# Two hyperbolic graph layers: four shared PSUM slots and two tiles per turn

## The chip, the cores and the metric

The kernel runs on one core of a Trainium2 chip. The metric is the device time in microseconds of one execution; for the kernel before the median of three runs is 863.87 us (863.44 to 865.81). The profile is of one further execution with a span of 859.7 us from first to last instruction.

## What is computed

Four graph layers run one after another on a node matrix `x` of 3327 x 64 with a 3327 x 3327 adjacency of zeros and ones. Each layer normalises the rows, cuts them at zero, applies a graph operation and adds its result to `x`. Layers 0 and 3 are hyperbolic and are the ones that the change touches. Cut to what matters (layer 0, c = 1):

```python
h = relu(layernorm(x))
left, right = logmap0(h) @ W[:64] + b, logmap0(h) @ W[64:]
att = sigmoid(left + right.T) * adj
local = logmap(h[:, None, :], h[None, :, :])       # 3327 x 3327 x 64 in the reference
x = x + proj(expmap(h, einsum('ij,ijd->id', att, local)))
```

The logarithmic map is a function of scalar products of two nodes times one of the two node vectors. So the kernel never builds the 64 components for a pair: it makes one number per pair of nodes, multiplies it by the attention weight, and sums it against the node vectors with matmuls.

## The kernel before

Rows are padded to 3328 = 26 x 128. In the kernel `T` is 26, `HT` 13 and `D` 64. `hyperbolic_series` is called twice: for layer 0, with the adjacency from memory in f32, and for layer 3, with masks in fp8 that layer 1 left on the chip. It has three stages: a preparation, a loop over pairs of nodes, and an end that makes the new `x`.

**Preparation** (L344 to L436). It normalises, makes `Xr` (scaled node vectors), splits it into f16 parts `hi` and `lo` beside nine columns `F` in the tile `Xp`, and transposes it 128 rows at a time with `to_columns16` into `XT` (high and low parts, one column per node). `Xe` and its transpose `XE` hold the other operand. `left` and `right` are the two terms of the attention; `left` is split into three bf16 parts and transposed into `LT`. `table_of` (L424) loads the sigmoid's function table.

**Loop** (L442 to L601). The result's columns are cut into four chunks: `(0, 4)`, `(4, 3)`, `(7, 3)`, `(10, 3)`, each of so many blocks of 128 columns in both halves of the nodes. A chunk is 2 x 512 or 2 x 384 columns wide, and for each chunk all 26 row blocks are gone through. So there are 26 wide tiles (128 x 1024) and 78 narrow ones (128 x 768) per loop. The order on the four computing engines is written out by hand, one tile a turn. Per tile, by name and line:

- `products` on TensorE, L519 and L520: four f16 matmuls make `L` in PSUM, from `XT` and `XE` (stationary) and from `XC` and `XF` (moving);
- `square` on ScalarE, L526: `y` from `L`;
- `sigmoid` on ScalarE, L504, from `leftB` (the chunk's `left`, the same in all partitions), then on GpSimd, L512, times the adjacency; in layer 0 the diagonal block of the adjacency is first cleared by `drop_diagonal` (L178), for 26 of the 104 tiles;
- `weights` on VectorE, L530 and L531: `L` becomes a series value, then `sig` becomes `L * sig`;
- `sums` on TensorE, L537: `sig` against `Xr`, summed over the 26 row blocks in PSUM; L545: after every second tile the same against `X0` for both tiles.

[...] `L` has two buffers of two banks each, so a tile's products wait until L531 of the tile two before has read its buffer. The two accumulators of a chunk take one bank each and have two buffers each. In turn k TensorE does `sums(k-2)` and then `products(k+1)`; ScalarE `square(k)` and `sigmoid(k+2)`; VectorE `weights(k)`.

What a chunk begins with is made in the turns before it: `columns` copies `XT` into `XC` by two DMAs (L473); `begin` spreads `left` over the partitions with matmuls (L480) into the coming chunk's accumulators, `begin2` copies that to `leftB` (L486) and transposes `Xp` into the same banks (L488), `begin3` copies that to `XF` (L494) and in layer 0 makes a part of `diag` on GpSimd (L497). What a chunk ends with is spread over turns after it: `out_of` (L554) copies the sums, `back` (L560) transposes them, `to_m` and `to_m2` (L567 to L576) reduce them.

Adjacency tiles come through SyncE's DMA queue (`load`, L467), with four buffers, issued three tiles ahead of the sigmoid. The same queue issues the `XC` copies.

Of the kernel before, what the change touches and what calls it, by code (L numbers as in the profile page):

```python
# [9 lines left out]
F32 = mybir.dt.float32  # L10
# [36 lines left out]
def tile_gnn4(ctx: ExitStack, tc: tile.TileContext, x, adjT, att0, b0, w1, bias1, w_gat, a_gat,  # L47
# [133 lines left out]
    def move(tp, hs, x2, m, s, q, r, min_norm2, um, maxn2, isqc):  # L181
# [80 lines left out]
        if isqc is not None:  # L262
# [8 lines left out]
    pick = const.tile([3 * T, T], BF, name="pick")  # L271
    V.memset(pick, 1.0)
    G.affine_select(out=pick, in_=pick, pattern=[[-3, T]], compare_op=OP.is_ge, fill=0.0,
                    base=0, channel_multiplier=1)
    G.affine_select(out=pick, in_=pick, pattern=[[3, T]], compare_op=OP.is_ge, fill=0.0,
                    base=2, channel_multiplier=-1)
# [31 lines left out]
    def hyperbolic_series(r, params, ok, masks=None, done=None):  # L308
# [15 lines left out]
        KE = D + 9  # L324
        W = 512
        with ExitStack() as st:
# [7 lines left out]
            XE = pers.tile([KE, NP], F16, name="XE")  # L334
            Xp = pers.tile([P, T, 2 * D + 9], F16, name="Xp")
            hi, lo, F = Xp[:, :, :D], Xp[:, :, D:2 * D], Xp[:, :, 2 * D:]
            LT = pers.tile([3 * T, P], BF, name="LT")
# [4 lines left out]
            wlr, bcol, cc, sqc, isqc, um, maxn2 = params  # L342

            with tc.tile_pool(name="hsp", bufs=1) as tp, tc.tile_pool(name="hsps", bufs=2, space=PSUM) as ps:  # L344
                A.memzero(X0)
                Xe = tp.tile([P, T, KE], F16, name="Xe")
                E = Xe[:, :, D:]
                V.memset(E[:, :, 6:], SX)
                for k, part in enumerate(f16_parts((1.0 - 2.0 * G1) * SX)):
                    V.memset(F[:, :, 6 + k:7 + k], part)  # L350
# [31 lines left out]
                root_ = sqrt_(tp, root, "zs")  # L382
                for ts in HALVES:
                    V.scalar_tensor_tensor(lo[:, ts, :], Xr[:, ts, :], SX, hi[:, ts, :], op0=OP.mult, op1=OP.subtract)  # L384
# [11 lines left out]

                to_columns16(XT, Xp[:, :, :2 * D], P, 1)

# [24 lines left out]
                pl = parts3(left, "pl", BF)  # L423
                table_of(AF.Sigmoid, root[:, :1])  # L424
                pe = ps.tile([P, 4 * P], F32, name="pe", bufs=1)
                PE.matmul(pe[:3 * T, :P], pl.rearrange("p t k -> p (t k)"), ident_bf, start=True, stop=True)
                A.activation(LT, pe[:3 * T, :P], AF.Copy)
                V.tensor_mul(right, lr[:, :, 1], z)
                V.tensor_scalar(right, right, bcol, None, op0=OP.add)
                for k, src in ((0, p0), (3, hm0), (5, h0)):  # L430
                    V.tensor_scalar(F[:, :, k:k + src.shape[-1]], src, -1.0, None, op0=OP.mult)
                to_columns16(XE, Xe, KE, 0)
# [9 lines left out]
            with tc.tile_pool(name="hsw", bufs=2) as wk, tc.tile_pool(name="hsps", bufs=2, space=PSUM) as ps, \  # L442
                    tc.tile_pool(name="hsacc", bufs=2, space=PSUM) as pa, \
                    tc.manual_schedule(engines={mybir.EngineType.Activation, mybir.EngineType.DVE,
                                                mybir.EngineType.PE, mybir.EngineType.Pool}):
                HT = T // 2
                tiles = [(c, b) for c in ((0, 4), (4, 3), (7, 3), (10, 3)) for b in range(T)]
                K = len(tiles)
                XC, XF = {}, {}
                acc, leftB, adjs, sigs, Ls, ys, later = {}, {}, {}, {}, {}, {}, {}  # L450

                def halves(t, c):

                    return t.rearrange("p (o i) -> p o i", o=2)[:, :, c[0] * P:(c[0] + c[1]) * P]
# [14 lines left out]
                def columns(c):  # L469

                    XC[c] = new("XC", c, F16)
                    for o in range(2):
                        nc.sync.dma_start(XC[c][o * D:(o + 1) * D, :, :], halves(XT[:D, :], c))  # L473

                def begin(c):
                    acc[c] = [pa.tile([P, W], F32, name=f"acc{o}") for o in range(2)]
                    for o in range(2):
                        for i in range(c[1]):
                            t = o * HT + c[0] + i
                            PE.matmul(acc[c][o][:, i * P:(i + 1) * P], pick[:, t:t + 1].to_broadcast([3 * T, P]), LT,  # L480
                                      start=True, stop=True)

                def begin2(c, o):
                    if o == 0:
                        leftB[c] = new("leftB", c)
                    A.activation(leftB[c][:, o, :], acc[c][o][:, :c[1] * P], AF.Copy)  # L486
                    for i in range(c[1]):
                        PE.matmul(acc[c][o][:KE, i * P:(i + 1) * P], Xp[:, o * HT + c[0] + i, D:], ident_h,  # L488
                                  start=True, stop=True)

                def begin3(c, o):
                    if o == 0:
                        XF[c] = new("XF", c, F16, KE)
                    A.activation(XF[c][:, o, :], acc[c][o][:KE, :c[1] * P], AF.Copy)  # L494
                    if masks is None:
                        t0 = o * HT + c[0]
                        G.tensor_tensor(diag[:, t0 * P:(t0 + c[1]) * P].rearrange("p (t i) -> p t i", i=P),  # L497
                                        ident[:, None, :].to_broadcast([P, c[1], P]),
                                        dcol[:, t0:t0 + c[1], None].to_broadcast([P, c[1], P]), op=OP.mult)

                def sigmoid(k):
                    c, b = tiles[k]
                    sig = sigs[k] = new("sig", c, bufs=6)
                    A.activation(sig, leftB[c], AF.Sigmoid, bias=right[:, b:b + 1])  # L504
                    if masks is None:
                        adj = adjs.pop(k)
                        t = b % HT - c[0]
                        if 0 <= t < c[1]:
                            drop_diagonal(adj[:, b // HT, t * P:(t + 1) * P], 0, 0, P)
                    else:  # L510
                        adj = halves(masks[b // 2][:, b % 2, :], c)
                    G.tensor_tensor(sig, adj, sig, op=OP.mult)  # L512

                def products(k):
                    c, b = tiles[k]
                    rows = slice(b * P, (b + 1) * P)
                    L = Ls[k] = ps.tile([P, 2, W], F32, name="L")[:, :, :c[1] * P]
                    for o in range(2):
                        PE.matmul(L[:, o, :], XT[:, rows], XC[c][:, o, :], start=True, stop=False)  # L519
                        PE.matmul(L[:, o, :], XE[:, rows], XF[c][:, o, :], start=False, stop=True)  # L520

                def square(k):

                    c, b = tiles[k]
                    ys[k] = new("y", c)
                    A.activation(ys[k], Ls[k], AF.Square, scale=-0.5 / SX ** 2, bias=shift_c)  # L526

                def weights(k):
                    L, y, sig = Ls.pop(k), ys.pop(k), sigs[k]
                    V.scalar_tensor_tensor(L, y, G3, L, op0=OP.add, op1=OP.mult)  # L530
                    V.tensor_mul(sig, L, sig)  # L531

                def sums(k):
                    c, b = tiles[k]
                    n = c[1] * P
                    for o in range(2):
                        PE.matmul(acc[c][0][o * D:(o + 1) * D, :n], Xr[:, b, :], sigs[k][:, o, :],  # L537
                                  start=b == 0, stop=b == T - 1)
                    if b % 2 == 1:

                        for i in range(2):
                            w = sigs.pop(k - 1 + i)
                            for o in range(2):
                                q = 32 * (2 * i + o)
                                PE.matmul(acc[c][1][q:q + 32, :n], X0[:, b - 1 + i, :], w[:, o, :],  # L545
# [994 lines left out]
```

## Time and profile before

| | |
|---|---|
| median of 3 runs | 863.87 us |
| span of the profiled execution | 859.7 us |
| VectorE busy | 728.3 us, 85% |
| TensorE busy | 672.2 us, 78% |
| ScalarE busy | 577.1 us, 67% |
| GpSimd busy | 425.7 us, 50% |
| DMA | 104.27 MB, mean 121 GB/s |

A line of the profile's groups names a source line, an engine, an operation, what it writes and reads, and how often it occurs; behind the bar stand the busy time in all, the mean time of one in ns, and the idle time of the engine just before these instructions with the instructions that ended most of it. In the timeline the columns are start, duration, engine, line and operation; brackets hold the idle time before and what ended it. PE is TensorE, DVE VectorE, ACT ScalarE, POOL GpSimd, SP SyncE. Durations of matmuls include the way through the array, so matmuls that follow each other overlap in the timeline, and the distance between starts is what one costs. The same holds, less so, for VectorE and ScalarE.

### The profile page before, as it was taken

Reading aid. Unit: us, or ns where it says so; the run is one execution under the profiler, and the core shown is the slowest. Engines: PE = TensorE matmul, PEld = TensorE weight load, DVE = VectorE, ACT = ScalarE, POOL = GpSimd, SP = SyncE. Lnnn points to the kernel's source line nnn. Section 1 sums busy time; section 2 is a strip of 40 time slices with the busy share of each in tenths; the row PEclk is TensorE's granted clock in tenths of the full one; section 3 lists DMA queues with packets and bytes.
Section 4 is the critical chain, followed back from the end, with each engine's and each line's share of the span. In section 5 each row is a group of like instructions: output and inputs, shape, how many; then the busy total and the mean of one; then the engine's idle time right before and its main releaser. Section 6 shows DMA issues by size and latency. Waiting matters only on the chain.

```text
span 859.7 us, 11940 instructions
## 1 busy us (share of the span) xinstructions
PE 672.2 (78%) x4264; PEld 245.2 (29%) x4264; DVE 728.3 (85%) x1020; ACT 577.1 (67%) x712; POOL 425.7 (50%) x309
## 2 busy tenths in 40 slices
PE   0489998989989219989990997617999899899960
PEld 0312232323322004434440562212222233232220
DVE  7389888889889899998989946795998889888976
ACT  3578878888978237777770306457888789788751
POOL 3289997998989410003110000005777677676730
PEclk9789999999999759999995899957999999999995
DMA  2556666666665428998944530001000000000001
GB/s 41 139 173 194 190 180 172 184 186 184 185 179 148 170 83 302 358 364 308 360 166 169 195 127 1 0 0 23 1 1 10 1 1 10 1 1 1 1 2 43
DMA packets 53877, 104.27 MB, mean 121 GB/s; under 512 B 8016, under 2 KB 30064, under 8 KB 53808
## 3 DMA queue, kind: packets, MB, share of 16 engines
q1 hardware_dynamic: 48704, 103.10, 37.8%
q10 hardware_dynamic: 4656, 0.08, 0.3%
q8 instruction: 35, 0.57, 0.3%
q14 instruction: 34, 0.28, 0.1%
q0 software_dynamic: 448, 0.24, 0.1%
HBM read 100.85 MB, written 0.85 MB: 118 GB/s over the span
## 4 chain that ended last, share of the span: by engine, by line
PE 46%; DVE 35%; ACT 11%; issue 4%; DMA 2%; ACTq 1%; DVEq 0%; SPq 0%; POOL 0%; POOLq 0%
DVE sig L531 11%; DVE L L530 10%; PE cnt L1265 9%; PE acc L537 7%; PE L L519 6%; PE acc L545 6%; ACT y L526 6%; PE acc L1282 5%; PE L L520 5%; PE acc L1378 4%; ACT sig L504 2%; DMA XC<-XT 1%; DVE deg L1397 1%; DVE X L711 1%; PE pt L391 1%
## 5 line engine op out<-in xcount | busy, mean ns | idle before, releaser
L512 POOL TENSOR_TENSOR sig<-mask,sig 128x768 f32<-128x768 fp8e4 (+1 forms) x104 | 174.5, 1679 | 215.7 <-DMA XC<-XT 153.4
L530 DVE SCALAR_TENSOR_TENSOR L<-y,L 128x768 f32<-128x768 f32 (+1 forms) x208 | 213.3, 1025 | 50.0 <-ACT y L526 48.0
L526 ACT ACTIVATE y<-L,shift_c 128x768 f32<-128x768 f32 (+1 forms) x208 | 198.1, 953 | 81.6 <-PE L L520 80.8
L531 DVE TENSOR_TENSOR sig<-L,sig 128x768 f32<-128x768 f32 (+1 forms) x208 | 213.2, 1025 | 21.7
L512 POOL TENSOR_TENSOR sig<-adj,sig 128x768 f32<-128x768 f32 (+1 forms) x104 | 202.6, 1960 | 27.5 <-ACT sig L504 22.4
L504 ACT ACTIVATE sig<-leftB,right 128x768 f32<-128x768 f32 (+1 forms) x208 | 203.7, 980 | 0.0
L537 PE MATMUL acc<-sig,Xr 128*64 128x384 f32 (+1 forms) x832 | 193.0, 542 | 2.1 <-DVE sig L531 2.1
L519 PE MATMUL L<-XC,XT 128*128 128x384 f16 (+1 forms) x416 | 146.5, 352 | 37.8 <-DVE sig L531 27.9
L520 PE MATMUL L<-XF,XE 73*128 73x384 f16 (+1 forms) x416 | 144.7, 348 | 0.0
L1271 ACT ACTIVATE w<-cnt,ebias 128x832 bf16<-128x832 f32 x104 | 93.7, 950 | 30.5 <-PE cnt L1265 30.5
L1178 DVE TENSOR_SCALAR_CACHE_REDUCE same<-adj 128x1664 bf16<-128x1664 f32 x52 | 97.7, 1879 | 3.1 <-DMA adj<-in 3.0
L519 PEld LDWEIGHTS <-XT 128*128 128x128 f16 x416 | 41.1, 99 | 198.1 <-DVE sig L531 154.7
L545 PE MATMUL acc<-sig,X 128*32 128x384 f32 (+1 forms) x832 | 94.2, 525 | 0.0
L1265 PE MATMUL cnt<-mask,after 128*128 128x416 fp8e4 x208 | 54.9, 347 | 23.3 <-DVE mask L1258 20.7
L178 POOL TENSOR_TENSOR mask<-mask,offdiag 128x128 fp8e4<-128x128 fp8e4 x26 | 13.4, 535 | 107.5 <-PE cnt L1265 105.5
L1265 PE MATMUL cnt<-mask,rest 128*128 128x416 fp8e4 x208 | 54.8, 346 | 12.4 <-ACT w L1271 12.4
L537 PEld LDWEIGHTS acc<-sig,Xr 128*64 128x64 f32 x832 | 41.3, 135 | 70.2 <-issue 63.9
L1258 DVE TENSOR_SCALAR mask<-adj 128x1664 fp8e4<-128x1664 f32 x52 | 53.3, 1033 | 1.4 <-DMA adj<-in 1.2
L1282 PE MATMUL acc<-w,h 128*64 128x416 bf16 x416 | 47.1, 349 | 0.0
L520 PEld LDWEIGHTS <-XE 73*128 73x128 f16 x416 | 41.5, 100 | 18.2 <-issue 2.2
L391 PE MATMUL pt<-ident_h,Xp 128*128 128x128 f16 x52 | 5.9, 313 | 41.5 <-DVE Xp L384 41.5
L1378 PE MATMUL acc<-mask,h 128*64 128x416 fp8e4 x416 | 37.9, 344 | 0.3
(295 smaller groups left out, 567.7 us busy)
## 6 DMA issues: line engine op xcount, KB each, us to landing
adj<-in SPq DMA_DIRECT2D x65, 832.0 KB, 6.4
adj<-in SPq DMA_DIRECT2D x78, 384.0 KB, 3.8
adj<-in SPq DMA_DIRECT2D x26, 512.0 KB, 4.7
XC<-XT SPq DMA_DIRECT2D x12, 96.0 KB, 2.6
X<-in SPq DMA_DIRECT2D x1, 832.0 KB, 4.5
out<-X SPq DMA_DIRECT2D x2, 416.0 KB, 2.7
XC<-XT SPq DMA_DIRECT2D x4, 128.0 KB, 5.1
gw<-in POOLq DMA_DIRECT2D x4, 48.0 KB, 6.4
```

The source lines that it names most:

```text
L504: A.activation(sig, leftB[c], AF.Sigmoid, bias=right[:, b:b + 1])
L512: G.tensor_tensor(sig, adj, sig, op=OP.mult)
L519: PE.matmul(L[:, o, :], XT[:, rows], XC[c][:, o, :], start=True, stop=False)
L520: PE.matmul(L[:, o, :], XE[:, rows], XF[c][:, o, :], start=False, stop=True)
L526: A.activation(ys[k], Ls[k], AF.Square, scale=-0.5 / SX ** 2, bias=shift_c)
L530: V.scalar_tensor_tensor(L, y, G3, L, op0=OP.add, op1=OP.mult)
L531: V.tensor_mul(sig, L, sig)
L537: PE.matmul(acc[c][0][o * D:(o + 1) * D, :n], Xr[:, b, :], sigs[k][:, o, :], start=b == 0, stop=b == T - 1)
L545: PE.matmul(acc[c][1][q:q + 32, :n], X0[:, b - 1 + i, :], w[:, o, :], start=b == 1, stop=b == T - 1, tile_position=(0, q))
L1178: V.tensor_scalar(same, adj, 0.0, 0.0, op0=OP.is_equal, op1=OP.add, accum_out=count)
L1265: PE.matmul(cnt[o][:, h, :BK], w, cols(k, o, h), start=w is after and steps[k][1] == T - 1, stop=True, skip_group_check=True)
L1271: A.activation(ws[k][:, o, :, :], cnt[o][:, :, :BK], AF.Exp, scale=-LN2, bias=ebias)
```

## The change

The loop is rebuilt around four PSUM slots of two banks each. At any time one is the running chunk's accumulator (both sums in one slot), up to three hold `L`; at the end of a chunk a slot is used to transpose the sums back. A slot that is done goes to the end of a list, and the next user takes the first. TensorE takes two tiles a turn: the sums of two tiles, then the products of two. A slot more for `L` is to let the products run further ahead of VectorE, and the larger turns to spare changes of operand on TensorE.

What a chunk begins with is no longer made by matmuls and copies in the loop. `XE` gets nine more rows that hold `F`, so that `XF` can be copied from `XT` and `XE` by DMA as `XC` is; `left` is written once to device memory as a row, and `leftB` is read from there into all partitions. The first chunk's operands can't wait for that: `XC` of that chunk is issued as soon as `XT` is whole, its `leftB` and `XF` are made in the preparation by matmuls and transposes, and the first adjacency loads and sigmoid are issued a tile earlier. `left` is transposed in f32 and no longer split. Ten matmuls without use (`keep_busy`) are to hold TensorE's clock up. The sigmoid's function table is loaded earlier.

`drop_diagonal` goes from this loop (for a pair of equal nodes the logarithmic map is zero). `sig` has seven buffers instead of six, `y` three instead of two.

```diff
-    pick = const.tile([3 * T, T], BF, name="pick")
...
+    rows = [nc.dram_tensor(f"left{k}", (T, P), F32, kind="Internal").ap() for k in range(2)]
...
+            def columns(c):
...
+                for o in range(2):
+                    nc.sync.dma_start(XC[c][o * D:(o + 1) * D, :, :], halves(XT[:D, :], c))
+                if c[0]:
+                    nc.sync.dma_start(XF[c][:D, :, :], halves(XT[D:, :], c))
+                    nc.sync.dma_start(XF[c][D:, :, :], halves(XE[KE:, :], c))
+                    nc.sync.dma_start(leftB[c], bass.AP(tensor=left_row.tensor, offset=left_row.offset + c[0] * P,
+                                                        ap=[[0, P], [HT * P, 2], [1, n]]))
...
+                table_of(AF.Sigmoid, root_[:, :1])
...
+                def keep_busy(n):
+
+                    for _ in range(n):
+                        PE.matmul(junk, ident_h, hi[:, :8, :], start=True, stop=True)
+
+                keep_busy(4)
                 to_columns16(XT, Xp[:, :, :2 * D], P, 1)
+                columns(chunks[0])
...
-                pl = parts3(left, "pl", BF)
-                table_of(AF.Sigmoid, root[:, :1])
...
+                PE.transpose(pe[:T, :P], left, ident)
+                A.activation(LT, pe[:T, :P], AF.Copy)
+                nc.sync.dma_start(left_row, LT)
+                c = chunks[0]
+                for o, to in ((0, junk), (1, pe)):
+                    for i in range(c[1]):
+                        t = o * HT + c[0] + i
+                        PE.matmul(to[:, i * P:(i + 1) * P], ident[:T, t:t + 1].to_broadcast([T, P]), LT,
+                                  start=True, stop=True)
+                    A.activation(leftB[c][:, o, :], to[:, :c[1] * P], AF.Copy)
...
-                to_columns16(XE, Xe, KE, 0)
+                G.tensor_copy(F, Fe)
+                to_columns16(XE, Xe, KE + 9, 0)
+                for o in range(2):
+                    pt = ps.tile([P, 4 * P], F16, name="pt", bufs=4)
+                    for i in range(c[1]):
+                        PE.transpose(pt[:KE, i * P:(i + 1) * P], Xp[:, o * HT + c[0] + i, D:], ident_h)
+                    V.tensor_copy(XF[c][:, o, :], pt[:KE, :c[1] * P])
+                keep_busy(6)
...
+                slots = [ps.tile([P, 2, W], F32, name=f"slot{k}") for k in range(4)]
+                made = [0]
...
-                    if masks is None:
-                        adj = adjs.pop(k)
-                        t = b % HT - c[0]
-                        if 0 <= t < c[1]:
-                            drop_diagonal(adj[:, b // HT, t * P:(t + 1) * P], 0, 0, P)
...
+                def products(to):
+
+                    while made[0] < min(to, K) and slots:
+                        k = made[0]
+                        made[0] += 1
+                        c, b = tiles[k]
+                        rows = slice(b * P, (b + 1) * P)
+                        L = Ls[k] = slots.pop(0)
...
                     V.scalar_tensor_tensor(L, y, G3, L, op0=OP.add, op1=OP.mult)
                     V.tensor_mul(sig, L, sig)
+                    slots.append(slot)
...
+                    if b == 0:
+                        acc[c] = slots.pop(0)
...
-                for k in range(-7, K + 10):
-                    if 0 <= k - 2 < K:
-                        sums(k - 2)
-                    if 0 <= k + 1 < K:
-                        products(k + 1)
...
+                for j in range(-1, K // 2 + 5):
+                    for k in (2 * j - 2, 2 * j - 1):
+                        if 0 <= k < K:
+                            sums(k)
+                    for i in range(2):
+                        k = 2 * j + i
+                        products(2 * j + 3 + i)
+                        if 0 <= k < K:
+                            weights(k)
+                        if i == 0 and (j, 0) in later:
+                            later.pop((j, 0))()
+                        products(2 * j + 4)
+                        if k + 2 < K:
+                            square(k + 2)
+                        if k + 3 < K:
+                            if masks is None and k + 5 < K:
+                                load(k + 5)
+                            sigmoid(k + 3)
+                        if i == 1 and (j, 1) in later:
+                            later.pop((j, 1))()
+                    if at(2 * j + 10, 1):
+                        columns(at(2 * j + 10, 1))
...
```

## The prediction

> **What bounds the kernel now.** First the busy shares: three engines are close together, so the page alone names no bound.
>
> ```profile
> PE 672.2 (78%) x4264; PEld 245.2 (29%) x4264; DVE 728.3 (85%) x1020; ACT 577.1 (67%) x712; POOL 425.7 (50%) x309
> PE 46%; DVE 35%; ACT 11%; issue 4%; DMA 2%; ACTq 1%; DVEq 0%; SPq 0%; POOL 0%; POOLq 0%
> ```
>
> The chain of work that ended last is mostly TensorE and VectorE, so I looked at where the two hyperbolic loops lie. By the timeline of VectorE the first runs from 44.11 (first L530) to 282.68 us (end of the last L531), 238.6 us; the second from 590.89 to 829.68, 238.8 us. Together 55% of the span. The changed lines lie in these loops and in the preparation before each.
>
> Next the groups by line, shapes apart: what one tile costs VectorE.
>
> ```profile
> L530 DVE SCALAR_TENSOR_TENSOR L<-y,L 128x768 f32<-128x768 f32 x156 | 149.6, 959 | 22.1 <-ACT y L526 20.3
> L531 DVE TENSOR_TENSOR sig<-L,sig 128x768 f32<-128x768 f32 x156 | 149.5, 958 | 16.3
> L530 DVE SCALAR_TENSOR_TENSOR L<-y,L 128x1024 f32<-128x1024 f32 x52 | 63.7, 1225 | 27.9 <-ACT y L526 27.7
> ```
>
> In the timeline two of these start 1.06 and 0.88 us apart (1.32 and 1.16 for 1024 columns), so VectorE can't do a narrow tile in under 1.94 us or a wide one in under 2.48. A loop has 26 wide and 78 narrow tiles: 64.5 + 151.3 = 216 us, with some 5 us of reductions between chunks 221. The loop takes 18 us more. The timeline of a steady stretch says why:
>
> ```profile
> 803.34 0.34 PE L519 MATMUL L<-XC,XT 128*128 128x384 f16 x1
> 804.11 0.87 PE L537 MATMUL acc<-sig,Xr 128*64 128x384 f32 x4
> 805.26 0.34 PE L519 MATMUL L<-XC,XT 128*128 128x384 f16 x1 [0.29 <-DVE sig L531]
> 806.02 0.87 PE L537 MATMUL acc<-sig,Xr 128*64 128x384 f32 x4
> 806.82 0.85 PE L545 MATMUL acc<-sig,X 128*32 128x384 f32 x8
> 807.60 0.34 PE L519 MATMUL L<-XC,XT 128*128 128x384 f16 x1
> 809.40 0.96 DVE L530 SCALAR_TENSOR_TENSOR L<-y,L 128x768 f32<-128x768 f32 x1 [0.30 <-ACT y L526]
> ```
>
> From start to start: products P 0.77, first sums S 0.80, second sums Z 0.78. A pair of tiles is P S P S Z, 3.92 us of TensorE; VectorE needs 3.88. Four tiles take 8.15 (801.25 to 809.40), 4.075 per pair: TensorE stands ready for P and waits for L531 to free one of only two L buffers (0.29), then P comes late, the square too, and VectorE waits (0.30). Two full engines wait for each other in turn. Wide pairs take 5.145 (10.29 for four). So 13 x 5.145 + 39 x 4.075 = 225.8; the remaining 12.9 us of a loop are its start and three chunk boundaries.
>
> Last the start of the first loop:
>
> ```profile
> 32.57 1.54 SPq L473 DMA_DIRECT2D XC<-XT  x2
> 34.16 6.93 SPq L467 DMA_DIRECT2D adj<-in  x3
> 41.04 0.61 PE L519 MATMUL L<-XC,XT 128*128 128x512 f16 x1 [7.88 <-DMA XC<-XT]
> 44.11 1.23 DVE L530 SCALAR_TENSOR_TENSOR L<-y,L 128x1024 f32<-128x1024 f32 x1 [14.00 <-ACT y L526]
> ```
>
> Everything stands from 33 to 41 us because XC was issued behind three adjacency loads of 512 KB. The 0.61 us matmul is one at half clock; the same shape takes 0.38 later.
>
> **What the Trainium skill says.** "VectorE: DVE Perf Modes" (Mode 1x): two tensor inputs in f32 go at one element per cycle of 0.96 GHz; 768 / 0.96 = 800 ns, and the trace's 959 with its fixed part agrees. The change leaves these operations alone, so the floor stays. "TensorE: Matmul & The Clock Gate" (The HAM clock gate): an idle array runs at half clock until some 3.4 us of activity; the trace agrees (0.61 against 0.38). "DMA: Bandwidth & Descriptors" (Queues, rings and completion order): each engine's ring takes descriptors in order, so a small copy waits behind big ones; the 7.88 us agrees. "ScalarE: Activation LUTs" (What ACT_TABLE_LOAD costs): 1283 ns; the trace has 1283.
>
> **The change part by part.**
>
> *Four slots.* One is the accumulator, three hold L. The order of a turn on TensorE becomes S(2j-2) S(2j-1) Z P(2j+2) P(2j+3). Call t0 the end of VectorE's tile 2j-1. S(2j-2) needs only tile 2j-2 and is done before t0. After it: S(2j-1), Z, P: 0.05 + 0.80 + 0.78 + 0.66 + 0.17 to the end of the last product = 2.46; the square (0.90) ends at t0 + 3.4, before VectorE wants tile 2j+2 at t0 + 3.88. P(2j+3) needs the slot of tile 2j, free at t0 + 1.94, and TensorE gets there at t0 + 2.29. Nobody waits. TensorE's own work: two P with one change of format (1.43), two S, Z: 3.81. ScalarE has 3.3 of work, GpSimd 3.64 (1.82 each): below 3.88. So VectorE sets the pair: 3.88, and since TensorE is only 0.07 below, I take 3.92. Wide: floor 4.96, TensorE about 4.86, taken 4.97. Loop: 13 x 4.97 + 39 x 3.92 = 217.5.
>
> *Chunk boundaries.* Removed: 6 to 8 L480 and L488 matmuls and four copies on ScalarE of 0.48 per chunk. Kept: out_of, back, to_m and the reductions, about 1.5 us of VectorE (2 after the wide chunk). New waits: the new accumulator takes the slot freed last, so the first S of a chunk waits for the second tile of the turn; behind it Z and P are late, the square ends at +4.25 and VectorE waits some 0.4. Two turns later back holds a slot, one P waits for the end of the turn (queued behind it: S and Z) and is made up within two turns. I take 2 us for a boundary, 3 for the first: 7. Loop: 224.5; saved 14.2.
>
> *Operands by DMA.* A later chunk brings XC, XF and leftB, some 700 KB, where one narrow adjacency load of 384 KB takes 3.8 us to land. In the instruction order of SyncE the XC and XF issues of a chunk stand behind the adjacency loads of the chunk before it, some 20 tiles (over 35 us) ahead of use; even four times 3.8 is hidden. The write of left (13 KB) stands 12 loads ahead of its first read. What waits behind these issues on SyncE is an adjacency load, and there are four buffers for it.
>
> *First chunk in preparation.* XC is issued once XT is whole (27.5 us instead of 32.57, with no big load ahead); it took 3.1 us in the second loop, where nothing was ahead of it (584.70 to 587.8): there at about 31. left goes through one transpose instead of five VectorE steps (1.2 us); leftB's two copies end at 31.5, the sigmoid at 32.7. The six extra keep_busy matmuls wait for the first leftB copy and hold up P(0): 6 x 0.22 = 1.3 us warm, 2.6 cold. P(0) from 32.4, square after the sigmoid at 33.4 to 34.5, L530 at 34.6. L531 also needs GpSimd's product with the first adjacency tile: issued near 30.5, landed by 33.6, product 2.36: 36.0, against 45.45. Saved 9.5. Second loop: leftB done near 585.4, XC near 585, keep_busy to 586.3 or 587.6, L530 at 588.4 to 589.7 against 590.89: saved 2.
>
> *GpSimd.* The 26 diagonal products of 0.46 go (12 us, in the first loop only). The two diag products of the first chunk (1.03 each) come between its early tiles; with 2.36 against VectorE's 2.48 this delays VectorE by some 1.5 us. Later ones (0.83) fit into the slack of 1 us.
>
> *Tail.* The last out_of may wait for Z of the same slot: 0.4 per loop as the middle of 0 and 0.8.
>
> Sum: 14.2 + 14.2 - 1.5 + 9.5 + 2 - 0.8 = 37.6; 863.9 - 37.6 = 826.3 us.
>
> **The rivals.**
>
> *R1, TensorE remains the bound.* If one S must follow another with a full drain, or the semaphore steps add up, a pair stays at 4.05 to 4.08. For it: 3.81 against 3.88 is thin. Against: the 0.29 idle before P is a wait for a buffer, not work. Then only the starts (9 and 1) and half of the boundaries (3 per loop) with a wide gain of 1 per loop remain: 18 us, 846.
>
> *R2, slower.* The slots run out: a products call that finds none is skipped, and with one L slot fewer the cycle S S Z P square pair is 8.1 us long for one turn (0.05 + 2.38 + 0.77 + 1.0 + 3.88) instead of for two. If only every seventh turn did this: 52 / 7 x 4.2 = 31 us per loop, less 37.6 once: 863.9 + 62 - 37.6 = 888. For it: the slots change roles at each boundary. Against: in the instruction order three L slots rotate throughout a chunk.
>
> *R3, VectorE never waits.* Loops at the floor of 221 (17.7 saved each), starts 10 and 3: 863.9 - 48.4 = 815.5. Against: boundaries and GpSimd's start.
>
> **How the numbers follow.** Forecast 0.60, R1 0.24, R3 0.09, R2 0.05, and 0.02 for no change (R1 with late transfers). The time is the forecast's, 826.3. The range runs from R3 (815) to just past R1 (848): it leaves out R2, no change and the worst of R1. Faster 0.92, same 0.02, slower 0.06.
>
> **What would show it.** Right: idle time before the L530 group falls from 50 us to under 20 and names ScalarE only near boundaries; four narrow tiles take 7.8 to 7.9; first L530 near 34.6; no DMA releaser in front of the first matmuls; DVE share rises to about 89%. Wrong: TensorE waits of 0.3 or more for L531 in every turn (R1: none, but PE over 97%), a DMA named as releaser at chunk starts, or GpSimd named before L531 throughout the first loop.

## The result and the profile after

The changed kernel takes 829.47 us, the median of four runs (828.18 to 831.17); the kernel before, beside it, 864.11 (863.44 to 865.81). The ratio is 0.9598 with a 95% interval of 0.9575 to 0.9620: 34.6 us less, where 37.6 were predicted.

The page of the changed kernel, its busy shares and the engines of the chain that ended last:

```profile
PE 662.2 (80%) x4228; PEld 251.2 (30%) x4228; DVE 721.5 (87%) x1013; ACT 562.0 (68%) x684; POOL 419.0 (51%) x283
DVE 65%; PE 14%; DMA 7%; ACT 6%; issue 5%; POOL 2%; ACTq 1%; DVEq 0%; POOLq 0%
```

VectorE does nearly the same work as before (721.5 against 728.3 us), but the chain is now 65% VectorE and 14% TensorE, where it was 35% and 46%. The groups by line say where VectorE's waits went (busy, mean ns, then idle before and its releasers):

```profile
L543 DVE TENSOR_TENSOR sig<-slot,sig 128x768 f32<-128x768 f32 (+1 forms) x208 | 213.2, 1025 | 24.7 <-POOL sig L519 2.7 <-DVE slot L542 0.9
L542 DVE SCALAR_TENSOR_TENSOR slot<-y,slot 128x768 f32<-128x768 f32 (+1 forms) x208 | 212.1, 1020 | 9.0 <-ACT y L537 8.9
```

L542 is the old L530, L543 the old L531. L530 waited 50.0 us over both shapes, almost all for the square; L542 waits 9.0. A steady stretch in the timeline (start, duration, engine and line):

```profile
140.84 0.95 DVE L542 SCALAR_TENSOR_TENSOR slot<-y,slot 128x768 f32<-128x768 f32 x1
...
141.90 0.96 DVE L543 TENSOR_TENSOR sig<-slot,sig 128x768 f32<-128x768 f32 x1
...
142.05 1.73 PE L552 MATMUL slot<-sig,Xr 128*64 128x384 f32 x8
...
142.77 0.95 DVE L542 SCALAR_TENSOR_TENSOR slot<-y,slot 128x768 f32<-128x768 f32 x1
...
143.71 0.85 PE L560 MATMUL slot<-sig,X 128*32 128x384 f32 x8
...
144.49 0.34 PE L530 MATMUL slot<-XC,XT 128*128 128x384 f16 x1
...
144.70 0.95 DVE L542 SCALAR_TENSOR_TENSOR slot<-y,slot 128x768 f32<-128x768 f32 x1
```

Three starts of L542 lie 1.93 us apart and no line has a bracket: a pair of tiles takes 3.86 us and VectorE never stops. Before, four tiles held a wait of 0.3 us on TensorE and one on VectorE. Wide pairs take 4.93.

By stages, from the first L542 (L530 before) and the end of the last L543 (L531) of each loop:

| us | before | after | change |
|---|---|---|---|
| start to first loop | 44.11 | 34.67 | -9.4 |
| first loop | 238.6 | 225.9 | -12.7 |
| between the loops | 308.2 | 311.9 | +3.7 |
| second loop | 238.8 | 224.3 | -14.5 |
| after the loops | 30.0 | 32.7 | +2.7 |
| span | 859.7 | 829.5 | -30.2 |

The profiled execution of the changed kernel was the slowest of its four, so the table shows less than the medians.

### The profile page after: what moved, and what is told of

Same layout as the page of the kernel before. It is cut to its first block, busy times and chain, and to the rows that moved or that the text cites. A ratio compares the mean times of both kernels' runs of the same rounds, so it can differ in the third digit from the quotient of the medians.

```text
span 829.5 us, 11810 instructions
## 1 busy us (share of the span) xinstructions
PE 662.2 (80%) x4228; PEld 251.2 (30%) x4228; DVE 721.5 (87%) x1013; ACT 562.0 (68%) x684; POOL 419.0 (51%) x283
## 4 chain that ended last, share of the span: by engine, by line
DVE 65%; PE 14%; DMA 7%; ACT 6%; issue 5%; POOL 2%; ACTq 1%; DVEq 0%; POOLq 0%
DVE sig L543 22%; DVE slot L542 20%; DMA adj<-in 7%; DVE same L1207 5%; PE acc L1407 5%; DVE mask L1287 3%; POOL sig L519 2%; PE slot L552 2%; ACT y L537 1%; DVE deg L1426 1%; PE cnt L1294 1%; DVE X L740 1%; DVE prod L739 1%; PE slot L560 1%; DVE ln_v L123 1%
## 5 line engine op out<-in xcount | busy, mean ns | idle before, releaser
L537 ACT ACTIVATE y<-slot,shift_c 128x768 f32<-128x768 f32 (+1 forms) x208 | 197.6, 950 | 69.7 <-ACT sig L517 48.1
L543 DVE TENSOR_TENSOR sig<-slot,sig 128x768 f32<-128x768 f32 (+1 forms) x208 | 213.2, 1025 | 24.7 <-POOL sig L519 2.7
L542 DVE SCALAR_TENSOR_TENSOR slot<-y,slot 128x768 f32<-128x768 f32 (+1 forms) x208 | 212.1, 1020 | 9.0 <-ACT y L537 8.9
L519 POOL TENSOR_TENSOR sig<-adj,sig 128x768 f32<-128x768 f32 (+1 forms) x104 | 201.8, 1962 | 24.8 <-ACT sig L517 14.7
L519 POOL TENSOR_TENSOR sig<-mask,sig 128x768 f32<-128x768 fp8e4 (+1 forms) x104 | 174.6, 1680 | 57.2 <-ACT sig L517 53.1
L552 PE MATMUL slot<-sig,Xr 128*64 128x384 f32 (+1 forms) x832 | 187.2, 538 | 18.3 <-DVE sig L543 18.3
L530 PE MATMUL slot<-XC,XT 128*128 128x384 f16 (+1 forms) x416 | 142.1, 342 | 5.0 <-DVE sig L543 3.3
L531 PE MATMUL slot<-XF,XE 73*128 73x384 f16 (+1 forms) x416 | 141.4, 340 | 0.0
L560 PE MATMUL slot<-sig,X 128*32 128x384 f32 (+1 forms) x832 | 95.0, 529 | 0.0
L552 PEld LDWEIGHTS slot<-sig,Xr 128*64 128x64 f32 x832 | 42.9, 135 | 123.9 <-DVE sig L543 85.2
L178 POOL TENSOR_TENSOR mask<-mask,offdiag 128x128 fp8e4<-128x128 fp8e4 x26 | 16.8, 666 | 105.4 <-PE cnt L1294 104.2
L530 PEld LDWEIGHTS <-XT 128*128 128x128 f16 x416 | 40.6, 98 | 94.7 <-issue 68.8
L1287 DVE TENSOR_SCALAR mask<-adj 128x1664 fp8e4<-128x1664 f32 x52 | 53.3, 1031 | 6.7 <-DMA adj<-in 6.6
L531 PEld LDWEIGHTS <-XE 73*128 73x128 f16 x416 | 40.7, 98 | 33.3 <-issue 9.3
```

Of the source, the lines that this page charges most:

```text
L530: PE.matmul(L[:, o, :c[1] * P], XT[:, rows], XC[c][:, o, :], start=True, stop=False)
L531: PE.matmul(L[:, o, :c[1] * P], XE[:KE, rows], XF[c][:, o, :], start=False, stop=True)
L537: A.activation(ys[k], Ls[k][:, :, :c[1] * P], AF.Square, scale=-0.5 / SX ** 2, bias=shift_c)
L552: PE.matmul(acc[c][o * D:(o + 1) * D, 0, :n], Xr[:, b, :], sigs[k][:, o, :], start=b == 0, stop=b == T - 1)
L560: PE.matmul(acc[c][q:q + 32, 1, :n], X0[:, b - 1 + i, :], w[:, o, :], start=b == 1, stop=b == T - 1, tile_position=(0, q))
```

## The experiments

Loops are measured as in the table. Each ratio is to the kernel before in the same session.

| run | us | ratio, 95% interval | loops, us |
|---|---|---|---|
| a1_two_slots | 831.84 | 0.9635, 0.9618 to 0.9651 | 226.3, 226.6 |
| a2_one_tile | 835.15 | 0.9675, 0.9652 to 0.9698 | 227.6, 226.0 |
| c1_two_real | 899.78 | 1.042, 1.0392 to 1.0449 | 260.2, 257.9 |
| c2_one_real | 858.23 | 0.9942, 0.9924 to 0.9960 | 239.1, 238.4 |
| b1_xc_first | 858.08 | 0.9938, 0.9922 to 0.9955 | 240.0, 238.8 |
| a3_no_busy | 829.82 | 0.9614, 0.9577 to 0.9651 | 226.8, 223.2 |
| d1_diag_prep | 828.87 | 0.9599, 0.9577 to 0.9621 | 226.1, 224.0 |
| d2_readers | 824.62 | 0.9555, 0.9530 to 0.9580 | 223.8, 221.1 |
| e1_busy_first | 823.59 | 0.9524, 0.9498 to 0.9549 | 223.7, 221.1 |
| e2_early_loads | 824.99 | 0.9539, 0.9522 to 0.9556 | 222.7, 221.5 |
| e3_drop_back | 835.74 | 0.9666, 0.9650 to 0.9683 | 230.5, 225.4 |
| e4_twice | 828.14 | 0.9575, 0.9555 to 0.9595 | 227.9, 224.1 |

### What ended the mutual wait

**At most two L tiles at once.**

```diff
-                    while made[0] < min(to, K) and slots:
+                    while made[0] < min(to, K) and slots and len(Ls) < 2:
```

> The changed kernel with at most two slots holding L at a time. Theory (the third L slot is what ends the mutual wait): the products of a turn's second tile then wait for the second L543 of the turn and stand ahead of the next sums, so turns of 3.9 and 5.0 us alternate: about 4.45 us per narrow pair and 5.6 per wide one against 3.86 and 4.93, some 30 us more per loop, 890 us in all (870 to 905). Rival (turns of two tiles and fewer operand changes carry the gain, the slot little): pairs stay within 0.1 us, 829 to 836 us.

Measured 831.84 us, narrow pairs at 3.86. The theory missed by 58 us, because the edit does not do what it was meant to: it limits how many tiles have a name at one time, but the list of slots is a queue, so P still takes the slot freed longest ago and three buffers still rotate. Only the boundaries feel it: around the first one, two pairs take 4.96 and 6.13 us instead of 4.55 and 5.82.

**One tile a turn, three buffers.**

```diff
-                for j in range(-1, K // 2 + 5):
-                    for k in (2 * j - 2, 2 * j - 1):
-                        if 0 <= k < K:
-                            sums(k)
-                    for i in range(2):
-                        k = 2 * j + i
-                        products(2 * j + 3 + i)
+                for k in range(-2, K + 10):
+                    j, i = k // 2, k % 2
+                    if 0 <= k - 2 < K:
+                        sums(k - 2)
+                    products(k + 3)
...
```

> The changed kernel with one tile per turn (sums of tile k-2, products of tile k+2, weights of tile k), but still three slots for L. Theory (slot): TensorE's work per narrow pair is 3.92 as before and nothing waits in a ring, so a pair takes 3.92 to 3.95 against 3.86: 836 us (831 to 840). Rival (the turn of two tiles carries the gain): pairs go back to 4.08 narrow and 5.15 wide, 23 us more, 852 us (847 to 858).

Measured 835.15, as the theory had it. TensorE's pair is now 3.90 us (first sums to first sums, 140.67 to 144.57 us) and VectorE's still 3.86: TensorE falls 0.04 behind per pair, uses up its lead within a chunk, and pays at the boundary (54.17, 53.93 and 53.66 us for the narrow chunks of the first loop against 53.33, 53.26 and 52.92). There it shows as VectorE waiting longer for ScalarE's L586, one of the readers of "The chunk ends": 1.53, 1.33 and 1.33 us before L591 instead of 0.59, 0.70 and 0.70. So the larger turns are worth about 5 us, with the readers in this order, and are not what ended the wait.

**Two buffers in turn, two tiles a turn.** The limit of a1, and:

```diff
                     V.tensor_mul(sig, L, sig)
-                    slots.append(slot)
+                    slots.insert(0, slot)
...
-                        acc[c] = slots.pop(0)
+                        acc[c] = slots.pop()
...
-                    slot = slots.pop(0)
+                    slot = slots.pop()
```

> Two buffers of the three hold L in turn, and P takes the one that VectorE freed last; the third free slot serves accumulators and transposes alone. Turn of two tiles as in the changed kernel. Theory (the third buffer in rotation is what ends the mutual wait; in the run with at most two L tiles named at once the three buffers still rotated, so it did not test this): the cycle from the end of one odd tile to the end of the next but one is 0.05 + 0.66 + 2.4 + 0.83 + 0.97 + 0.1 + 3.88 = 8.9 us for four tiles, 4.44 a narrow pair against 3.86, wide about 5.66 against 4.93; 0.58 x 78 + 0.73 x 26 = 64, so about 893 us (870 to 900), slower than the kernel before. Rival (the order S S Z P P is enough, whatever the buffers): pairs stay at 3.86, 832 us.

Measured 899.78: slower than before the change, narrow pairs mostly 3.92 and 4.92 in alternation, 4.51 and 4.32 in the third chunk (mean 4.42 in both, expected 4.44), wide 4.94 and 6.24. The timeline of this run:

```profile
142.00 0.32 PE L530 MATMUL slot<-XC,XT 128*128 128x384 f16 x1 [0.21 <-DVE sig L543]
...
143.94 0.32 PE L530 MATMUL slot<-XC,XT 128*128 128x384 f16 x1 [1.11 <-DVE sig L543]
...
144.68 1.51 PE L552 MATMUL slot<-sig,Xr 128*64 128x384 f32 x8
```

TensorE stands 1.11 us with sums ready behind a P that waits for the second tile's buffer; then come two sums in a row and the next P is late.

**Two buffers in turn, one tile a turn.** Both edits.

> The same two buffers in turn, with one tile per turn of TensorE (S P S Z P); everything else as in the changed kernel. Theory (buffers set the wait): with the first sums, the second sums and a product in a row, 0.77 + 0.80 + 0.78 = 2.35 us stand against VectorE's 1.94, the next P comes 0.4 late and the square with it; a narrow pair takes 4.1 to 4.2 us, as before the change, and the time is 854 us (848 to 864): the whole gain in the loops goes, the gain of the starts stays. Rival (with the copies and matmuls of the chunk starts gone, two buffers suffice): pairs 3.9, 833 to 836 us as with one tile per turn alone.

Measured 858.23, narrow pairs 3.92 and 4.27 (mean 4.10), wide 4.97 and 5.36; the loops take 239.1 and 238.4 us, what they took before the change. The group of TensorE's products in the kernel before (L519), and in the changed kernel, c1 and c2 (L530):

```profile
L519 PE MATMUL L<-XC,XT 128*128 128x384 f16 (+1 forms) x416 | 146.5, 352 | 37.8 <-DVE sig L531 27.9 <-DMA XC<-XT 8.8
```

```profile
L530 PE MATMUL slot<-XC,XT 128*128 128x384 f16 (+1 forms) x416 | 142.1, 342 | 5.0 <-DVE sig L543 3.3 <-ACT sum L570 0.7 <-ACT M L592 0.4
```

```profile
L530 PE MATMUL slot<-XC,XT 128*128 128x384 f16 (+1 forms) x416 | 144.2, 347 | 82.4 <-DVE sig L543 79.9
```

```profile
L530 PE MATMUL slot<-XC,XT 128*128 128x384 f16 (+1 forms) x416 | 143.8, 346 | 36.6 <-DVE sig L543 35.8
```

The products' wait for L543 (L531 before) is 3 us in all with three buffers in rotation, and 28, 80 and 36 with two. In one-tile turns the third buffer is worth 858.23 - 835.15 = 23 us, in two-tile turns 899.78 - 831.84 = 68. With two buffers the larger turn would have cost 42 us. c1 and c2 keep the rest of the change, the operands by DMA, seven `sig` and three `y` buffers; with two buffers for L these bring the loops nothing. Whether the third buffer would do as much without them was not run.

### The starts

**XC ahead of the adjacency, in the kernel before.**

```diff
-                if masks is None:
-                    for k in range(3):
-                        load(k)
                 columns(tiles[0][0])
+                if masks is None:
+                    for k in range(3):
+                        load(k)
```

> The kernel before, with XC of the first chunk issued ahead of the three adjacency loads instead of behind them, nothing else. Theory (the queue behind 1.5 MB is what cost the start of the first loop): first L530 near 37 us instead of 44.1, second loop unchanged, 857 us (854 to 859). Rival (GpSimd's first product then waits for its adjacency tile, or leftB and XF set the start): first L531 moves by less than 3 us, 861 us or more.

Measured 858.08, 5 us less, and its timeline has XC first:

```profile
30.43 1.33 SPq L473 DMA_DIRECT2D XC<-XT  x2
31.80 8.21 SPq L467 DMA_DIRECT2D adj<-in  x5
...
33.60 0.61 PE L519 MATMUL L<-XC,XT 128*128 128x512 f16 x1 [0.49 <-DMA XC<-XT]
```

The first L530 moves from 44.11 to 36.84 us. The first L531, which also needs GpSimd's product with the adjacency, moves less, from 45.45 to 39.47 us: a part of the rival came true, and the first loop takes 1.4 us longer. In the changed kernel the two stand at 34.67 and 36.01 us. Of 9.4 us that the change gains at the first weights to be finished, the order of two DMA issues gives 6.0; preparing the first chunk early, with its loads and sigmoid a tile earlier, gives the other 3.5.

**Without keep_busy.**

```diff
-                keep_busy(4)
...
-                keep_busy(6)
```

> The changed kernel without its ten keep_busy matmuls. Theory (in these starts TensorE has work enough, and the six hold up the first products): first L542 0.9 us earlier in the first loop, at most 1 us later in the second, total 829 us (826 to 831). Rival (without them the array runs at half clock into the loop): products at 0.61 us in the first turns of both loops, L542 some 1 to 3 us later in each, 833 us (831 to 836).

Measured 829.82: nothing that can be told from 829.47. The first loop's first product goes from 32.37 to 33.10 us, and products are at half clock. The timelines of a3 and of the changed kernel:

```profile
33.94 0.63 PE L529 MATMUL slot<-XF,XE 73*128 73x512 f16 x1
```

```profile
33.04 0.38 PE L531 MATMUL slot<-XF,XE 73*128 73x512 f16 x1
```

From the preparation's first reduction of `x2` to the first weights it took 19.70 us instead of 18.64 there, but 18.22 instead of 19.50 before the second loop. (The text of the next run names the second reduction; the distances are from the first of the two.) The next run asks whether that second difference is real.

**keep_busy in the first preparation alone**, with the readers' order of d2 below.

```diff
-                keep_busy(4)
+                if masks is None:
+                    keep_busy(4)
```

and the same for `keep_busy(6)`.

> The four readers in the new order, as in the run before, and the ten matmuls without use kept in the first preparation alone. Theory (they spare 1.06 us before the first loop, where TensorE would otherwise be at half clock, and cost 1.25 us before the second, where they stand between leftB and the first products: distances from the second reduction of x2 to the first L542 of 18.64 against 19.70 us and of 19.47 against 18.22 us with and without them): the second start becomes 18.2 us, the first stays at 18.6, and the time falls from 824.6 to 823.4 us. Rival (the difference was chance): second start 19.5 us, 824.6 us.

Measured 823.59 with an interval that overlaps that of d2: undecided by the time. By the trace the theory fell: the second start took 20.15 us, with products at 0.63 us, half clock. Without the extra matmuls this start took 18.22, 20.15 and 20.03 us (a3, e1, e2): the clock rises in time in one execution and not in another. With them it took 19.45 to 19.50 in all nine profiles. They buy evenness there, not time, and the evenness doesn't last: from the same reduction to the first weights of the second chunk it took 83.6 to 85.8 us in the seven profiles with them and three buffers, and 82.3, 84.2 and 84.1 without, because in five of those seven the second pair of tiles was held up (see the last section).

### GpSimd and the transfers

**diag of the first chunk in the preparation.** The two products move behind `G.tensor_copy(F, Fe)`:

```diff
+                if masks is None:
+                    for o in range(2):
+                        t0 = o * HT
+                        G.tensor_tensor(diag[:, t0 * P:(t0 + 4) * P].rearrange("p (t i) -> p t i", i=P),
...
-                            if at(2 * j + 2 - 2 * o, 0):
-                                make_diag(at(2 * j + 2 - 2 * o, 0), o)
+                            if at(2 * j + 2 - 2 * o, 1):
+                                make_diag(at(2 * j + 2 - 2 * o, 1), o)
```

> The two diag products of the first chunk move from GpSimd's stream among the first tiles to the preparation of the first loop, where GpSimd is idle. Theory: the waits of 0.56, 1.06 and 0.96 us for GpSimd before L543 near 44, 47 and 51 us go, the loop's first pair stays, and the time falls by 2 to 2.6 us, to 827 us. Rival: VectorE is then held by the third or fourth load of the adjacency or by the squares, and less than 1 us is gained.

Measured 828.87; the first chunk takes 66.62 us (66.36 in the changed kernel): by these numbers the rival holds. GpSimd's first instructions in this run, and VectorE's longest wait in the chunk:

```profile
34.54 7.01 POOL L525 TENSOR_TENSOR sig<-adj,sig 128x1024 f32<-128x1024 f32 x3 [8.14 <-DMA adj<-in]
41.81 2.37 POOL L525 TENSOR_TENSOR sig<-adj,sig 128x1024 f32<-128x1024 f32 x1 [0.25 <-DMA adj<-in]
45.37 2.35 POOL L525 TENSOR_TENSOR sig<-adj,sig 128x1024 f32<-128x1024 f32 x1 [1.19 <-DMA adj<-in]
```

```profile
47.58 1.23 DVE L548 SCALAR_TENSOR_TENSOR slot<-y,slot 128x1024 f32<-128x1024 f32 x1 [2.02 <-ACT y L543]
```

With the products gone GpSimd waits for the adjacency, but of these waits only the first reaches VectorE (0.45 us before the first L549). What holds VectorE is the rival's other half, a square that comes 2.02 us late: TensorE had a granted clock of 0.50 from 40.0 to 46.8 us in this execution, and of 1.00 there in the profile of the changed kernel. So what the move is worth at the full clock is not shown.

**diag and the loads together**, on top of e1: the products as in d1, and four loads right after `columns(chunks[0])`, with `adj` in the outer pool.

```diff
                 columns(chunks[0])
+                if masks is None:
+                    for k in range(4):
+                        load(k)
```

> As the run before it in this list, and the first chunk's diag products in the preparation, and the first four loads of the adjacency issued right after XC, some 2 us earlier and ahead of the write of left. Theory (with diag out of the way GpSimd waited 0.45, 0.25 and 1.19 us in the first tiles for adjacency loads, so both have to go together): the first chunk of the first loop falls from 66.3 to about 64.3 us, as in the second loop, and the time to 821.5 us. Rival (the fifth and sixth load wait for a buffer that GpSimd frees, which moves with GpSimd, so an early start of the first four gains nothing): 65.5 us or more, 823 us.

Measured 824.99, not to be told from e1. In the trace the waits for the adjacency are gone, and the first chunk takes 65.2 us instead of 66.2; what is left is a wait of 1.03 us for a square. In the profile, though, the preparation itself began 2 us later (first reduction at 18.10 instead of 16.16 us); whether the edit has a part in that was not tried.

**The diagonal products back on GpSimd.**

```diff
+                    t = b % HT - c[0]
+                    if masks is None and 0 <= t < c[1]:
+                        drop_diagonal(adj[:, b // HT, t * P:(t + 1) * P], 0, 0, P)
```

> The changed kernel with the 26 products of 0.46 us that clear the diagonal blocks back on GpSimd in the first loop. Theory (GpSimd has 1.82 of VectorE's 1.94 us per narrow tile and 2.36 of 2.47 per wide one, so a product every fourth tile or less overruns the slack of 0.1 us a tile where they follow one another): the diagonal blocks come in runs of 3 or 4 successive tiles, twice a chunk; sig runs some tiles ahead, which takes up part; 12 us more on GpSimd, 3 to 8 us more in the time, 833 to 837 us. Rival (the lead takes up all of it): within 1 us of 829.5.

Measured 835.74: 6 us more, of which the first loop shows 4.6. The group of L543 (L546 in this run):

```profile
L546 DVE TENSOR_TENSOR sig<-slot,sig 128x768 f32<-128x768 f32 (+1 forms) x208 | 213.2, 1025 | 29.3 <-POOL sig L522 8.5 <-DVE slot L545 0.9
```

VectorE waits 8.5 us for GpSimd instead of 2.7. Work on an engine that is half idle over the span cost about 5 of its 12 us, because in this stage the engine has 0.1 us of slack per tile. In the kernel before, where VectorE was slower per tile, the same products cost nothing that shows: the loop with them took 238.6 us, the one without 238.8.

**Operands of later chunks read twice.**

```diff
-                if c[0]:
+                for _ in range(2 if c[0] else 0):
```

> The changed kernel with each later chunk's XF and leftB read twice, one read behind the other, some 600 KB more per chunk. Theory (the transfers lie more than 35 us ahead of use, and four adjacency buffers cover the queue): within 1 us of the changed kernel, 829.5 us. Rival (the adjacency loads behind them in the queue come late for GpSimd in the first loop): 1 to 3 us at each of three boundaries of the first loop, 833 us or more, and a DMA named before L519 there.

Measured 828.14, within 1.4 us of the changed kernel; by the list of transfers one reading is 384 KB of `leftB` and 110 of `XF`, so 490 KB more per chunk rather than 600. The transfers are hidden, but perhaps not by much: at one boundary of six VectorE waited 1.59 us for GpSimd, and that chunk took 55.1 us instead of 53.3. GpSimd had stood 0.98 us just before, with the sigmoid that it needs already done, so a late adjacency load is likely; the trace does not name it.

### The chunk ends

**Readers grouped by engine.**

```diff
                     V.tensor_mul(prod[:, 0], by_tiles(Xr, c), pm)
+                    V.reduce_sum(by_tiles(M0, c), pm0[:, :, :, :, 0], axis=AX.X)
                     A.activation(prod[:, 1], pm, AF.Square)
+                    A.activation(by_tiles(M, c), pm, AF.Copy)
+                    slots.append(slot)
...
-                    V.reduce_sum(by_tiles(M0, c), pm0[:, :, :, :, 0], axis=AX.X)
-                    A.activation(by_tiles(M, c), pm, AF.Copy)
-                    slots.append(slot)
```

> After the transposes the four readers of the slot run VectorE, VectorE, ScalarE, ScalarE in one step instead of VectorE, ScalarE, VectorE, ScalarE in two. Theory (readers of one slot wait for one another even when they read different banks, so each change of engine costs a hop and a wait in order): the tail from the last L543 to the end of the last sums of a loop falls from 5.4 to about 4.6 us, VectorE loses its wait of 0.6 at each of six boundaries; 3 to 5 us in all, 825 us. Rival (the order of readers costs nothing, the tail is the transposes): within 1 us of the changed kernel.

Measured 824.62, 4.9 us less than the changed kernel. The end of the second loop in the changed kernel, in the timeline:

```profile
797.63 0.85 PE L560 MATMUL slot<-sig,X 128*32 128x384 f32 x8
798.55 0.87 ACT L570 ACTIVATE sum<-slot 128x384 f32<-128x384 f32 x2 [4.43 <-PE slot L560]
799.09 0.93 PE L579 MATMUL slot<-ident,sum 128*128 128x128 f32 x6 [0.61 <-ACT sum L570]
800.06 0.55 DVE L585 TENSOR_TENSOR prod<-Xr,slot 128x384 f32<-128x384 f32 x1 [3.28 <-PE slot L579]
800.64 0.49 ACT L586 ACTIVATE prod<-slot 128x384 f32<-128x384 f32 x1 [1.22 <-DVE prod L585]
801.17 0.17 DVE L591 TENSOR_REDUCE M<-slot 128x6 f32<-128x12 f32 x1 [0.56 <-ACT prod L586]
801.37 0.49 ACT L592 ACTIVATE M<-slot 128x384 f32<-128x384 f32 x1 [0.24 <-DVE M L591]
```

Of the four readers of the slot (L585, L586, L591, L592) each after the first names the one before it as its releaser. The Trainium skill has a reason for the first of these three waits, L586 behind L585, which read the same bank: "PSUM — Partial Sum Buffer" (PSUM bank collisions raise a hardware error) says that two engines may not access one bank at once, two readers included, and that the compiler adds a dependency between them. L591, however, reads the other bank of the slot and still waits 0.56 us for L586, and L592, back on the first bank, 0.24 us for L591; here the order is kept for the whole slot. With the new order:

```profile
793.61 0.56 DVE L585 TENSOR_TENSOR prod<-Xr,slot 128x384 f32<-128x384 f32 x1 [3.28 <-PE slot L579]
794.08 0.16 DVE L587 TENSOR_REDUCE M<-slot 128x6 f32<-128x12 f32 x1
...
794.34 0.49 ACT L588 ACTIVATE prod<-slot 128x384 f32<-128x384 f32 x1 [1.36 <-DVE M L587]
794.72 0.48 ACT L589 ACTIVATE M<-slot 128x384 f32<-128x384 f32 x1
```

One change of engine instead of three. The narrow chunks of the first loop take 52.65, 52.58 and 52.24 us in place of 53.33, 53.26 and 52.92, and those of the second gain as much: 0.68 at each of six boundaries, 4.1 us. The ends of the two loops give 0.4 and 0.3 more (first use of all the reductions, L645, 5.35 and 5.46 us after the last L543 instead of 5.73 and 5.77). This is the version to keep; it beats both kernels, and nothing added to it was shown to be faster still.

## Why the prediction was right, point by point

*The bound.* Right: two buffers made two nearly full engines wait for each other. The second rival's cycle was not: it put a turn of two tiles with one slot fewer at 8.1 us, and c1, which has one buffer fewer in rotation throughout, takes 4.42. The 4.44 that fits is c1's own expectation.

*Pairs.* 3.92 and 4.97 were predicted as an allowance above VectorE's floor; 3.86 and 4.93 came, even a little under the floor of 3.88 and 4.96 that had been read from start distances. 78 narrow and 26 wide pairs in both loops: 78 x 0.06 + 26 x 0.04 = 5.7 us better than predicted.

*Loops.* 224.5 each plus 1.5 of GpSimd in the first; measured 225.9 and 224.3. The sum hits because two misses cancel: the pairs were better, and the boundaries and first tiles worse. Boundaries were put at 3, 2 and 2 us; by the pairs' excess over steady ones they took 3.1, 2.7 and 2.6 (the second of the first loop: 4.22 + 4.40 + 5.66 less 3 x 3.86). What was not priced is the order of the readers, 0.68 each.

*First start.* 34.6 predicted, 34.67 measured; L543 at 36.0 and 36.01.

*Second start.* 2 us predicted, 1.0 measured (20.51 to 19.50 us from the reduction of `x2`). The first product came at the late end of what was given for the matmuls without use: 17.20 us after the reduction, and 15.93 without them (a3).

*GpSimd.* VectorE's waits near 44, 47 and 51 us are 2.6 in sum against 1.5 predicted. The first and the third, 0.56 and 0.96, follow a diag product and make the 1.5; the 1.06 between them follows 1.04 us in which GpSimd itself waited for an adjacency load, which the prediction did not have. It also gave no price to the removal of the diagonal products: e3 shows that without it the new loop would be 4.6 us longer.

*Tail.* 0.4 per loop predicted, 1.5 measured (from the last L543 to L644 5.40 us, before 3.88 to L615). Of this 0.8 is the copy that waits for the second sums in the same slot (L570 begins 1.77 us after VectorE's end, before 0.96), the upper end of what was given, and 0.2 more has come by the first reader (L585 at 3.28 us, L567 at 2.29). The other 0.5 lies among the readers, and d2's order gives 0.3 to 0.4 of it back.

*Not predicted.* Of the 3.7 us between the loops 1.5 are the tail and -1.0 the second start; 3.2 are left. Much of that may be spread: over all fourteen profiles this stretch took 308.2 to 313.1 us, and 310.6 in b1, where none of its code was changed. After the last VectorE instruction the program took 1.2 us longer (6.1 and 6.3 us with the old loop, 7.2 to 7.8 with the new one, but 5.8 in e4). No computing engine works there; its cause stays open.

In the profiled execution, then: -37.6 predicted, -5.7 for the pairs, +3.0 for boundaries, +2.5 for the first tiles of both loops (225.9 and 224.3 less 214.6 of pairs and 8.5 of boundaries, 4.0, against 1.5; 1.05 of it is the wait for a square at half clock that the last section shows), +2.2 for the tails, +1.0 for the second start, +3.2 and +1.2 not predicted: -30.2, as in the table. The median is 1.7 us better than the profiled execution of the changed kernel, and 2.6 worse than that of the kernel before, which makes the 34.6.

*Signs.* Of those that were named, the idle time before the first weights (9.0 us), the first start and the first products without a wait for a DMA came as said. Four narrow tiles took 7.72 us instead of 7.8 to 7.9, and VectorE's share rose to 87% instead of 89%.

## What to carry to other kernels

When two engines are each near full and hand tiles to each other, as VectorE and TensorE do here, two buffers can make them wait in turn; count the buffers that rotate, not the tiles that have a name. Check an experiment's own mechanism in its trace: a1 looked like a refutation and had taken nothing away. After such a change, look at the short serial ends, since the order of four small readers was worth more here than any further start-up trick. And ask of an engine with idle time how much of it lies in the stage that gets faster: GpSimd had room for the diagonal products only as long as VectorE waited.

## What the runs showed of the hardware

TensorE's clock fell again inside a running loop. Windows of the changed kernel at the start of the second loop (stretch, its length, then PE, PEld, DVE, ACT and POOL busy, granted clock, DMA share, GB/s):

```profile
572.00:576.00 4.00, 2.75 (x13) 0.80 (x11) 3.44 (x3) 4.00 (x5) 2.83 (x3) 1.00 0.06 21
576.00:580.00 4.00, 2.62 (x10) 0.43 (x12) 3.79 (x5) 3.52 (x4) 3.96 (x3) 0.71 0.00 0
580.00:584.00 4.00, 4.00 (x22) 1.10 (x16) 2.85 (x3) 1.68 (x2) 1.61 (x1) 0.87 0.00 0
```

and the timelines of the changed kernel and of d2 at the second tile's sums:

```profile
577.54 1.90 PE L552 MATMUL slot<-sig,Xr 128*64 128x512 f32 x4 [1.39 <-DVE sig L543]
...
583.46 1.23 DVE L542 SCALAR_TENSOR_TENSOR slot<-y,slot 128x1024 f32<-128x1024 f32 x1 [1.05 <-ACT y L537]
```

```profile
574.27 1.08 PE L552 MATMUL slot<-sig,Xr 128*64 128x512 f32 x4 [1.39 <-DVE sig L543]
```

Two idle stretches of 1.25 and 1.39 us while the first tiles pass through VectorE were followed by half clock in one execution (0.71 as the mean of 4 us, the second tile's sums 1.90 us) and not in the other (1.08 us); it cost VectorE 1.05 us. "TensorE: Matmul & The Clock Gate" (The HAM clock gate) says that the activity windows run freely and that the same kernel therefore differs from run to run; the traces agree. It leaves 1 us or two of each start to chance: the second pair of the second loop took between 4.93 and 7.03 us in the profiles with three buffers.
